# A state-space block and an FP4 feed-forward on one core: the rounded activations turned by DMA in bfloat16, their scales turned apart and repeated through DRAM

## The chip, the cores and the metric

The kernel runs on one core of a Trainium2 chip (trn2). The metric is device time in microseconds (us) for one launch. The kernel before takes 2007.83 us, the median of three runs that lie between 2003.05 and 2008.29 us. The profile was taken from one further execution, which took 2006.57 us.

## The reference

The input x is 8 sequences of 2048 tokens with 256 channels. The first half is a simplified Mamba layer (`xz = x @ W_in`, a causal convolution of 4 taps over 512 channels, SiLU, a small projection to 16 states, a mean over the sequence, a gate `silu(z)`, `@ W_out`), followed by a residual and a LayerNorm. The second half, which the change touches, is a gated feed-forward whose operands are all rounded to FP4 in blocks of 16 along the contraction:

```python
def fp4_quant_dequant(x):                       # blocks of 16 along the last dim
    scale = max(max|xb| / 6, 1e-12)
    return GRID[searchsorted(MID, |xb / scale|)] * sign(xb) * scale
def fp4_linear(x, w): return einsum('bsk,nk->bsn', fp4(x), fp4(w))
h = silu(fp4_linear(x, w_gate)) * fp4_linear(x, w_up)      # 256 -> 704
out = layernorm(x + fp4_linear(h, w_down))                 # 704 -> 256
```

So every activation that enters a feed-forward matmul is a grid value (at most 6, exact in bfloat16) times one scale for its block of 16.

## The kernel before, in words

**Tiles.** The sequence is cut into blocks of 512 tokens (`begin_block`, 32 of them), and each block into two pairs of 128-token tiles (`finish_pair`, 64 of them, m = 0 to 63). A block does the input projection (L408), the convolution taps on VectorE (L423), the state projection (L434) and its sums. `mix_block` (L521) adds the state's part four blocks later (`LAG = 4`). A pair does the gate branch z (L571), the output projection (L589), residual and LayerNorm, then the feed-forward: gate and up (L623), their product `h` (L638), down (L660), residual, LayerNorm, store.

**Rounding.** `quantize` (L164) has four steps. `scales` takes the maximum of each block (L180), a negative scale `nsc` (L184) and its reciprocal (L186), on VectorE. `normalize` multiplies on VectorE (L192) and takes the magnitude in bfloat16 on ScalarE (L199). `add` and `subtract` (L204, L208) round to the grid on VectorE. Last, GpSimd multiplies the rounded values by their scale (L209), in float32, in the layout [token, channel]. It is used for x1 (the LayerNorm's output, 2 x 256 columns a pair) and for h (2 x 704 = 1408 columns a pair), and for the three weights once.

**Turning.** TensorE contracts over partitions, so x1 and h must have channels on partitions. `turn_xq` (L604) makes four 128x128 TensorE transposes (L610) and one ScalarE copy out of PSUM (L612) for each pair. `turn_h` (L642) makes ten full transposes (L649) and two for the last 64 channels of each token tile (L652), with ScalarE copies L650 and L653. `down` (L655) then has twelve matmuls, six chunks of channels for each of two token tiles.

**Order.** Each step is put in a list by `at(place, f)`, where the places are constants at the top of the file (`GATE`, `QUANT2`, `HT`, `DOWN` ...), 64 of them to a block and 32 to a pair. The list is sorted and run, and a scheduler in the framework settles each engine's final order. Engines then work in order and wait on semaphores. All DMAs are issued from SP (SyncE), in order too. PSUM has seven banks in rotation (`bank`, L161). The drain at the end holds the four blocks of lag: there only pairs are left.

**Around the change.** `h`, the rounding scratch `q_x` and the convolution's `acc` have two or three buffers, and `x1`, `xq`, `r2` are separate tiles.

Of the kernel before, what the change touches and what calls it, by code (L numbers as in the profile page):

```python
# [8 lines left out]
F32 = mybir.dt.float32  # L9
BF16 = mybir.dt.bfloat16  # L10
# [17 lines left out]
CONV = (0.1, 17.0, 27.7, 51.2)  # L28
CONV_TAPS = 0.6
XPROJ = 66.0  # L30
TOKEN = 81.9
SOFTPLUS = 84.9
TURN = (75.4, 87.8, 88.5, 88.7)
SUMS = 93.4
SUM_LAG = 4.1
SKIP = 93.5
SKIP_STEP = 1.6
ZED = (24.8, 30.3)
MIX = 40.5
MIX_LAG = 2.2  # L40
MIX_STEP = 2.4
GATED = 13.9
GATED_LAG = 5.2
OUT = 59.5
NORM1 = 60.8
NORM_STEP = 4.3
QUANT1 = 86.5
QUANT1_STEP = 0.4
XQ = 90.2
GATE = (100.5, 104.5, 105.4)  # L50
PRODUCT_LAG = 5.5
QUANT2 = 118.6
QUANT2_STEP = 6.3
HT = 138.3
DOWN = 150.8
NORM2 = 160.8
PREPARE = (18.2, 50.1, 111.5, 171.7)
# [3 lines left out]
def mamba_fp4_ffn_kernel(  # L61
# [40 lines left out]
    ps_h = ctx.enter_context(tc.tile_pool(name="ps_h", bufs=1, space=PSUM))  # L102

# [16 lines left out]
    wdT = const.tile([P, NF + 1, DM], F32, name="wdT")  # L120

    hqT_of = [const.tile([P, NT * (NF + 1), P], F32, name=f"hqT{i}") for i in range(2)]
# [5 lines left out]
    nc.gpsimd.memset(wdT[TAIL:, NF, :], 0.0)  # L128
    for hqT in hqT_of:
        nc.gpsimd.memset(hqT[TAIL:, NT * NF :, :], 0.0)  # L130
# [33 lines left out]
    def quantize(place, v, q, n, step):  # L164

        nb = n // BLK
        state = {}

        def by_block(a):
            return a.rearrange("p (g k) -> p g k", k=BLK)

        def scales():
            amax = small.tile([P, nb], F32, tag="q_amax", name="q_amax")
            nc.vector.tensor_reduce(  # L180
                amax, by_block(v()), AX.X, ALU.max, apply_absolute_value=True
            )
            nsc = small.tile([P, nb], F32, tag="q_sc", name="q_sc")
            nc.vector.tensor_scalar(nsc, amax, -SIXTH, -1e-12, ALU.mult, ALU.min)  # L184
            rs = small.tile([P, nb], F32, tag="q_rs", name="q_rs")
            nc.vector.reciprocal(rs, nsc)  # L186
            state.update(nsc=nsc, rs=rs)

        def normalize():
            size, bufs = (T, 2) if n <= T else (NT * FF, 1)  # L190
            xn = fp4.tile([P, size], F32, tag=f"q_x{size}", name="q_x", bufs=bufs)[:, :n]
            nc.vector.tensor_tensor(  # L192
                by_block(xn),
                by_block(v()),
                state["rs"].unsqueeze(2).to_broadcast([P, nb, BLK]),
                ALU.mult,
            )
            w = fp4.tile([P, size], BF16, tag=f"q_w{size}", name="q_w", bufs=bufs)[:, :n]
            nc.scalar.activation(w, xn, AF.Abs, scale=GRID)  # L199
            state.update(x=xn, w=w)  # L200

        def add():
            xn, w = state["x"], state["w"]
            nc.vector.scalar_tensor_tensor(xn, w, 1.5 * GRID, xn, ALU.max, ALU.subtract)  # L204

        def subtract():
            xn, w = state["x"], state["w"]
            nc.vector.scalar_tensor_tensor(w, w, 1.5 * GRID, xn, ALU.max, ALU.subtract)  # L208
            nc.gpsimd.tensor_tensor(  # L209
                by_block(q()),  # L210
                by_block(w),
                state["nsc"].unsqueeze(2).to_broadcast([P, nb, BLK]),
                ALU.mult,
            )

        for i, f in enumerate((scales, normalize, add, subtract)):
            at(place + i * step, f)

    def prepare_gate_up(place, w, wT):
        wv = {}  # L220

        def load():
            wv["w"] = p2.tile([P, NF, DM], F32, tag="h", name="wv")
            nc.sync.dma_start(wv["w"], w[: NF * P, :].rearrange("(j p) d -> p j d", p=P))
# [5 lines left out]
        quantize(place + 0.5, flat, flat, NF * DM, 1.0)  # L230
# [18 lines left out]
    def prepare_gate_up_tail(place):  # L249
# [3 lines left out]
        def load():  # L253
            wv["w"] = p2.tile([P, DM], F32, tag="h", name="wt")
            nc.sync.dma_start(wv["w"][:TAIL], w_gate[NF * P :, :])
            nc.sync.dma_start(wv["w"][TAIL:], w_up[NF * P :, :])

        at(place, load)
        quantize(place + 0.5, lambda: wv["w"], lambda: wv["w"], DM, 0.5)
# [17 lines left out]
    def prepare_down(place):  # L277
        wv = {}

        def load():  # L280
            wv["w"] = p2.tile([P, KM, FF], F32, tag="h", name="wdv")
            nc.sync.dma_start(wv["w"], w_down.rearrange("(r p) f -> p r f", p=P))

        def flat():
            return wv["w"].rearrange("p r f -> p (r f)")

        at(place, load)
        quantize(place + 0.5, flat, flat, KM * FF, 1.0)

        def turn(r):  # L290
            cols = slice(r * P, (r + 1) * P)
            for j0, j1 in ((0, 4), (4, NF)):
                tp = bank()
                for j in range(j0, j1):
                    nc.tensor.transpose(
                        tp[:, (j - j0) * P : (j - j0 + 1) * P],
                        wv["w"][:, r, j * P : (j + 1) * P],
                        ident,
                    )
                nc.scalar.copy(  # L300
                    wdT[:, j0:j1, cols],
                    tp[:, : (j1 - j0) * P].rearrange("p (j n) -> p j n", n=P),
                )
            tp = bank()
            nc.tensor.transpose(tp[:TAIL, :P], wv["w"][:, r, NF * P :], ident)
            nc.scalar.copy(wdT[:TAIL, NF, cols], tp[:TAIL, :P])

        for r in range(KM):
            at(place + 9.0 + 2 * r, turn, r)
# [77 lines left out]
    def begin_block(n):  # L387
# [9 lines left out]
        def project(c):  # L397
# [3 lines left out]
            xp = s["xp"] = p3.tile([P, HALO + T], F32, tag="xp", name="xp")  # L401
# [16 lines left out]
            acc = s["acc"] = p3.tile([P, T], F32, tag="acc", name="acc")  # L418
            nc.scalar.activation(acc, xp[:, 0:T], AF.Copy, scale=cw_sb[:, c, 0:1])  # L419

        def tap(c, k):
            acc, xp = s["acc"], s["xp"]
# [3 lines left out]
            if k == KC - 1:  # L426
                nc.scalar.activation(s["xc"][:, c, :], acc, AF.Silu, bias=cb_sb[:, c : c + 1])  # L427
# [120 lines left out]
    def finish_pair(m):  # L548
# [52 lines left out]
        def make_xq():  # L601
            q["xq"] = p2.tile([P, NT * DM], F32, tag="xq", name="xq")

        def turn_xq():  # L604
            tp = bank()
            xq = q["xq"].rearrange("p (t d) -> p t d", d=DM)
            for k in range(KM):
                for t in range(NT):
                    o = k * U + t * P
                    nc.tensor.transpose(tp[:, o : o + P], xq[:, t, k * P : (k + 1) * P], ident)  # L610
            q["xqT"] = p2.tile([P, KM, U], F32, tag="xqT", name="xqT")
            nc.scalar.copy(q["xqT"].rearrange("p k t -> p (k t)"), tp)  # L612

        def gate_up(f0):
            if f0 == 0:
                q["h"] = p2.tile([P, NT, FF], F32, tag="h", name="h")
            n = min(FW, FF - f0)
            gu = []
            for wT in (wgT, wuT):
                mm = bank().rearrange("p (t n) -> p t n", n=FW)  # L620
                for t in range(NT):
                    for k in range(KM):
                        nc.tensor.matmul(  # L623
                            mm[:, t, :n],
                            q["xqT"][:, k, t * P : (t + 1) * P],
# [16 lines left out]
        def turn_h():  # L642
            h, hT = q["h"], hqT_of[m % 2]
            cols = [h[:, t, j * P : (j + 1) * P] for t in range(NT) for j in range(NF)]
            for j0 in range(0, len(cols), 4):
                j1 = min(j0 + 4, len(cols))
                tp = bank().rearrange("p (j n) -> p j n", n=P)
                for j in range(j0, j1):
                    nc.tensor.transpose(tp[:, j - j0, :], cols[j], ident)  # L649
                nc.scalar.copy(hT[:, j0:j1, :], tp[:, : j1 - j0, :])  # L650
            for t in range(NT):
                nc.tensor.transpose(tp[:TAIL, NT + t, :], h[:, t, NF * P :], ident)  # L652
            nc.scalar.copy(hT[:TAIL, NT * NF :, :], tp[:TAIL, NT:, :])  # L653

        def down():  # L655
            hT = hqT_of[m % 2]
            mm = q["d"] = bank().rearrange("p (t n) -> p t n", n=DM)
            for t in range(NT):
                for j in range(NF + 1):
                    nc.tensor.matmul(  # L660
                        mm[:, t, :],
                        hT[:, t * NF + j if j < NF else NT * NF + t, :],
                        wdT[:, j, :],
# [4 lines left out]
        def residual2():  # L668
            q["r2"] = p2.tile([P, NT, DM], F32, tag="r2", name="r2")
            nc.vector.tensor_tensor(q["r2"], q["x1"], q["d"], ALU.add)  # L670

        def store():
            nc.sync.dma_start(of[b, i], q["r2"])
# [3 lines left out]
        for j in range(2):  # L677
# [5 lines left out]
        at(base + QUANT1 - 0.1, make_xq)  # L683
        quantize(
            base + QUANT1,
            lambda: q["x1"].rearrange("p t d -> p (t d)"),
            lambda: q["xq"],
            NT * DM,
            QUANT1_STEP,
        )  # L690
        at(base + XQ, turn_xq)
# [7 lines left out]
        quantize(base + QUANT2, flat, flat, NT * FF, QUANT2_STEP)  # L699
        at(base + HT, turn_h)  # L700
        at(base + DOWN, down)
        at(base + NORM2, residual2)
        layernorm(base + NORM2 + 0.5, lambda: q["r2"], lambda: q["r2"], NORM_STEP)
# [11 lines left out]
    prepare_down(PREPARE[3])  # L715
# [49 lines left out]
```

## Time and profile before

| | |
|---|---|
| runs, median (range) | 2007.83 us (2003.05 to 2008.29) |
| the profiled execution, whole | 2006.57 us |
| its span | 2004.6 us |
| TensorE matmuls (PE) busy | 1952.9 us, 97% |
| TensorE weight loads (PEld) | 1586.8 us, 79% |
| VectorE (DVE) | 1534.9 us, 77% |
| ScalarE (ACT) | 992.8 us, 50% |
| GpSimd (POOL) | 663.3 us, 33% |
| DMA, mean share of 16 engines | 11.1%, 72.92 MB moved |
| TensorE clock granted | 0.992 of full |

The span runs from the first to the last instruction, and the remaining 2 us lie around it. A busy time is the union of an engine's instructions. The profile's matmul rows give pipelined durations whose ends are modelled, so a matmul's share of time is better read from the starts of neighbours in the timeline than from its mean. Each float32 matmul instruction of the program appears as two records in it, a transpose as one. In the groups, `out<-in` names the tiles, the number after x counts instructions, and what follows the second bar is the idle time of the engine ahead of them with what ended it.

### The profile page before, as it was taken

To read this page: it belongs to the slowest core of one execution; us is meant where nothing else is said; L and a number is where in the kernel's file an instruction comes from. 1 tells how busy PE (TensorE), PEld (TensorE's weight loads), DVE (VectorE), ACT (ScalarE), POOL (GpSimd) and SP (SyncE) were. 2 spreads that over 40 slices of the span, in tenths; PEclk is the share of its full clock that TensorE was granted. 3 is DMA by queue.
4 is the path that set the end of the run, shared out by engine and by line. 5 is a ranking of instruction groups with operands and counts; after the bars stand their busy time and mean duration, and the time that the engine had idled before them with its cause. 6 is when DMAs were issued, how large, how long until landed. Compare 5 with 4: busy or idle time off the path is not lost.

```text
span 2004.6 us, 31117 instructions
## 1 busy us (share of the span) xinstructions
PE 1952.9 (97%) x12146; PEld 1586.8 (79%) x12146; DVE 1534.9 (77%) x2938; ACT 992.8 (50%) x1764; POOL 663.3 (33%) x658
## 2 busy tenths in 40 slices
PE   5799999999999999999999999999999999999997
PEld 2468888888888888888888888888888888888886
DVE  6878777887777877777777777777777877767775
ACT  4755545455544455444455444555445555433332
POOL 2224323423333323333233432333323333333331
PEclk8999999999999999999999999999999999999998
DMA  4011111101111110011011011011011011011100
GB/s 129 32 39 36 32 38 43 38 32 32 32 38 43 34 36 32 27 43 43 29 35 39 27 43 43 27 33 43 27 43 40 30 33 32 17 32 32 37 13 20
DMA packets 66290, 72.92 MB, mean 36 GB/s; under 512 B 6112, under 2 KB 57184, under 8 KB 66144
## 3 DMA queue, kind: packets, MB, share of 16 engines
q1 hardware_dynamic: 66144, 70.94, 11.1%
q8 instruction: 96, 1.57, 0.3%
q14 instruction: 50, 0.41, 0.1%
HBM read 54.15 MB, written 16.78 MB: 35 GB/s over the span
## 4 chain that ended last, share of the span: by engine, by line
PE 93%; DVE 4%; POOL 1%; ACT 1%; issue 0%; DMA 0%; SPq 0%; POOLq 0%; ACTq 0%; DVEq 0%
PE ps L623 31%; PE ps L660 16%; PE ps L571 11%; PE ps L589 11%; PE ps L408 10%; PE ps L649 3%; PE ps L434 3%; PE ps L465 2%; PE ps L532 2%; PE hsum L475 2%; PE ps L610 1%; DVE acc L423 1%; PE ps L652 1%; DVE q_x L192 0%; DVE q_amax L180 0%
## 5 line engine op out<-in xcount | busy, mean ns | idle before, releaser
L660 PE MATMUL ps<-wdT,hqT 128*128 128x256 f32 x1536 | 345.9, 380 | 0.5 <-ACT hqT L650 0.3
L623 PE MATMUL ps<-wgT,xqT 128*128 128x256 f32 (+1 forms) x1536 | 341.7, 365 | 0.7 <-ACT xqT L612 0.7
L623 PE MATMUL ps<-wuT,xqT 128*128 128x256 f32 (+1 forms) x1536 | 335.6, 361 | 0.0
L660 PEld LDWEIGHTS ps<-wdT,hqT 128*128 128x128 f32 x1536 | 288.6, 190 | 51.6 <-issue 6.2
L623 PEld LDWEIGHTS ps<-wgT,xqT 128*128 128x128 f32 x1536 | 276.4, 190 | 39.7 <-ACT x L373 5.0
L423 DVE SCALAR_TENSOR_TENSOR acc<-xp,cw_sb,acc 128x512 f32<-128x512 f32 x384 | 288.4, 753 | 24.3 <-ACT acc L419 11.1
L623 PEld LDWEIGHTS ps<-wuT,xqT 128*128 128x128 f32 x1536 | 279.5, 190 | 26.5
L408 PE MATMUL ps<-xT,w_in_sb 128*128 128x512 f32 x512 | 254.0, 603 | 6.2 <-DMA xT<-in_x_t_dram 6.2
L571 PE MATMUL ps<-xTz,w_in_sb 128*128 128x256 f32 x1024 | 245.0, 382 | 0.0
L589 PE MATMUL ps<-w_out_sb,xc 128*128 128x256 f32 x1024 | 231.6, 379 | 0.0
L571 PEld LDWEIGHTS ps<-xTz,w_in_sb 128*128 128x128 f32 x1024 | 189.9, 190 | 48.6 <-issue 25.3
L582 POOL TENSOR_TENSOR xc<-xc,sz 128x512 f32<-128x512 f32 x128 | 166.2, 1309 | 154.7 <-ACT sz L578 88.9
L632 ACT ACTIVATE sg<-ps 128x512 f32<-128x512 f32 (+1 forms) x192 | 106.7, 556 | 217.9 <-PE ps L623 217.9
L589 PEld LDWEIGHTS ps<-w_out_sb,xc 128*128 128x128 f32 x1024 | 189.6, 190 | 23.2
L427 ACT ACTIVATE xc<-acc,cb_sb 128x512 f32<-128x512 f32 x128 | 92.4, 722 | 222.5 <-DVE acc L423 222.5
L209 POOL TENSOR_TENSOR h<-q_w,q_sc 128x1408 f32<-128x1408 bf16 x64 | 165.4, 2584 | 107.1 <-DVE q_w L208 82.8
L204 DVE SCALAR_TENSOR_TENSOR q_x<-q_w,q_x 128x1408 f32<-128x1408 bf16 (+2 forms) x132 | 153.2, 1160 | 56.9 <-ACT q_w L199 56.5
L638 DVE TENSOR_TENSOR h<-sg,ps 128x512 f32<-128x512 f32 (+1 forms) x192 | 122.8, 640 | 89.3 <-PE ps L623 86.6
L405 POOL COPY xp<-halo 128x3 f32<-128x3 f32 x96 | 78.6, 818 | 323.2 <-DVE acc L423 175.1
L578 ACT ACTIVATE sz<-ps 128x512 f32<-128x512 f32 x128 | 75.8, 592 | 184.9 <-PE ps L571 184.9
L199 ACT ACTIVATE q_w<-q_x 128x1408 bf16<-128x1408 f32 (+2 forms) x132 | 132.3, 1003 | 56.5 <-DVE q_x L192 53.8
L208 DVE SCALAR_TENSOR_TENSOR q_w<-q_w,q_x 128x1408 bf16<-128x1408 bf16 (+2 forms) x132 | 153.5, 1163 | 0.6
(101 smaller groups left out, 2586.9 us busy)
## 6 DMA issues: line engine op xcount, KB each, us to landing
xT<-in_x_t_dram SPq DMA_DIRECT2D x32, 512.0 KB, 3.6
xTz<-in_x_t_dram SPq DMA_DIRECT2D x64, 256.0 KB, 2.9
xt<-in_L_attn_x_dram SPq DMA_DIRECT2D x64, 256.0 KB, 2.7
out_dram<-r SPq DMA_DIRECT2D x64, 256.0 KB, 2.1
w_in_sb<-in_L_attn_W_in_dram SPq DMA_DIRECT2D x2, 512.0 KB, 4.2
wdv<-in_L_ffn_w_down_dram SPq DMA_DIRECT2D x1, 704.0 KB, 4.1
wv<-in_L_ffn_w_gate_dram SPq DMA_DIRECT2D x1, 640.0 KB, 6.9
wv<-in_L_ffn_w_up_dram SPq DMA_DIRECT2D x1, 640.0 KB, 9.2
```

The source lines that it names most:

```text
L199: nc.scalar.activation(w, xn, AF.Abs, scale=GRID)
L204: nc.vector.scalar_tensor_tensor(xn, w, 1.5 * GRID, xn, ALU.max, ALU.subtract)
L208: nc.vector.scalar_tensor_tensor(w, w, 1.5 * GRID, xn, ALU.max, ALU.subtract)
L209: nc.gpsimd.tensor_tensor(by_block(q()), by_block(w), state["nsc"].unsqueeze(2).to_broadcast([P, nb, BLK]), ALU.mult,)
L408: nc.tensor.matmul(mm, w_in_sb[:, k, c * P : (c + 1) * P], s["xT"][:, k, :], start=(k == 0), stop=(k == KM - 1),)
L423: nc.vector.scalar_tensor_tensor(acc, xp[:, k : k + T], cw_sb[:, c, k : k + 1], acc, ALU.mult, ALU.add)
L571: nc.tensor.matmul(mm[:, j, :], w_in_sb[:, k, DI + (c + j) * P : DI + (c + j + 1) * P], q["xT"][:, k, :], start=(k == 0), stop=(k == KM - 1),)
L582: nc.gpsimd.tensor_tensor(xc, xc, q["sz"][:, c : c + 2, :], ALU.mult)
L589: nc.tensor.matmul(mm[:, t, :], s["xc"][:, c, o : o + P], w_out_sb[:, c, :], start=(c == 0), stop=(c == NC - 1),)
L623: nc.tensor.matmul(mm[:, t, :n], q["xqT"][:, k, t * P : (t + 1) * P], wT[:, k, f0 : f0 + n], start=(k == 0), stop=(k == KM - 1),)
L638: nc.vector.tensor_tensor(q["h"][:, :, f0 : f0 + n], sg[:, :, :n], up[:, :, :n], ALU.mult)
L660: nc.tensor.matmul(mm[:, t, :], hT[:, t * NF + j if j < NF else NT * NF + t, :], wdT[:, j, :], start=(j == 0), stop=(j == NF),)
```

## The change

- `quantize` is split. Its rounding becomes `round_fp4`, and the weights still use it with the GpSimd multiply as before. x1 and h use a new `quantize_turned`.
- There the rounded, unscaled grid values (bfloat16) are turned by one DMA transpose from SBUF to SBUF (4 blocks of 128 columns for x1, 11 for h).
- The scales, [128 tokens, 32 or 88 blocks], are turned by one small TensorE transpose and copied out of PSUM by ScalarE. One DMA writes them to DRAM 16 times each, a second DMA reads them back so that each channel's partition has the scale of its block.
- GpSimd then multiplies on the turned side, float32 scales with bfloat16 values.
- `turn_xq` and `turn_h` are gone. h is turned as 11 whole chunks over the two token tiles, so the middle chunk holds the last 64 channels of the first tile and the first 64 of the second; `wdT` becomes two tiles, one for each token tile, padded with zero rows to fit. `down` keeps twelve matmuls. The down weights are prepared in two halves.
- `h` and `q_x` get one buffer each, `acc` is worked in place in `xc`, and the second residual is made in place in `x1`.
- All places at the top of the file have new values.

```diff
+    dram = ctx.enter_context(tc.tile_pool(name="dram", bufs=2, space=bass.MemoryType.DRAM))
...
-    wdT = const.tile([P, NF + 1, DM], F32, name="wdT")
+    wdT = [const.tile([P, NF + 1, DM], F32, name=f"wdT{t}") for t in range(NT)]
...
+    def quantize_turned(place, v, n, step, spread_lag, turn_lag, qT):
+        state = round_fp4(place, v, n, step)
+        nb, chunks = n // BLK, n // P
+        def turn_scales():
+            tp = bank()
+            nc.tensor.transpose(tp[:nb, :P], state["nsc"], ident)
+            scT = p2.tile([P, P], F32, tag="q_scT", name="q_scT")
+            nc.scalar.copy(scT[:nb, :], tp[:nb, :P])
+            rows = dram.tile([nb, BLK, P], F32, tag=f"q_rows{n}", name="q_rows")
+            nc.sync.dma_start(rows, scT[:nb, :].unsqueeze(1).to_broadcast([nb, BLK, P]))
+            state["rows"] = rows
+        def spread_scales():
+            state["scT"] = fp4.tile([P, chunks, P], F32, tag=f"q_s{n}", name="q_s", bufs=1)
+            nc.sync.dma_start(
+                state["scT"], state["rows"].rearrange("(c b) k n -> (b k) c n", c=chunks)
+            )
+        def turn():
+            state["gT"] = fp4.tile([P, chunks, P], BF16, tag=f"q_gT{n}", name="q_gT", bufs=1)
+            nc.sync.dma_start_transpose(state["gT"], state["g"])
+        def scale():
+            nc.gpsimd.tensor_tensor(qT(), state["gT"], state["scT"], ALU.mult)
...
-        def turn_xq():
...
-                    nc.tensor.transpose(tp[:, o : o + P], xq[:, t, k * P : (k + 1) * P], ident)
...
-                            q["xqT"][:, k, t * P : (t + 1) * P],
+                            q["xqT"][:, t * KM + k, :],
...
-        def turn_h():
...
-                    nc.tensor.transpose(tp[:, j - j0, :], cols[j], ident)
...
-                        hT[:, t * NF + j if j < NF else NT * NF + t, :],
-                        wdT[:, j, :],
+                        q["hqT"][:, t * NF + j, :],
+                        wdT[t][:, j, :],
```

## The prediction

> **What bounds the kernel now.** I read the engines' busy shares first, then busy time by stretch, then the groups of instructions with shapes kept apart, then TensorE's timeline in a steady stretch and at the end, and last the DMA issues.
>
> ```profile
> span 2004.6 us, 31117 instructions
> PE 1952.9 (97%) x12146; PEld 1586.8 (79%) x12146; DVE 1534.9 (77%) x2938; ACT 992.8 (50%) x1764; POOL 663.3 (33%) x658
> PE   5799999999999999999999999999999999999997
> ```
> ```profile
> 512.00:1024.00 512.00, 512.00 (x3224) 418.56 (x3224) 394.58 (x767) 258.40 (x461) 174.41 (x170) 1.00 0.11 35
> ```
>
> The columns of the second fence are length, then PE, PEld, DVE, ACT and POOL, clock, DMA share. In the middle PE has no gap at all (512.00 of 512.00) at full clock, while DVE works 77% and the DMA engines 11%. PE is idle only at the head (36.7 us in the first 128, from the same view's rows) and at the end (15 us in the last 85). So a PE instruction removed from the middle is time removed, as long as nothing new arrives late.
>
> ```profile
> L649 PE MATMUL ps<-ident,h 128*128 128x128 f32 x640 | 81.5, 275 | 6.2 <-POOL h L209 6.2
> L610 PE MATMUL ps<-ident,xq 128*128 128x128 f32 x256 | 38.5, 273 | 0.0
> L652 PE MATMUL ps<-ident,h 128*64 128x128 f32 x128 | 25.4, 280 | 0.1
> L209 POOL TENSOR_TENSOR h<-q_w,q_sc 128x1408 f32<-128x1408 bf16 x64 | 165.4, 2584 | 107.1 <-DVE q_w L208 82.8 <-DVE sp_acc L332 14.8 <-DVE sp_acc L337 5.8
> L582 POOL TENSOR_TENSOR xc<-xc,sz 128x512 f32<-128x512 f32 x128 | 166.2, 1309 | 154.7 <-ACT sz L578 88.9 <-DVE xc L542 59.5 <-DVE ln_mv L361 4.1
> ```
> ```profile
> 1014.87 1.25 PE L649 MATMUL ps<-ident,h 128*128 128x128 f32 x10
> 1015.96 0.60 PE L465 MATMUL ps<-ident,xc 128*128 128x128 f32 x4
> ...
> 1026.78 0.60 PE L610 MATMUL ps<-ident,xq 128*128 128x128 f32 x4
> 1027.21 3.62 PE L589 MATMUL ps<-w_out_sb,xc 128*128 128x256 f32 x16
> ```
>
> A transpose's mean of 275 ns overlaps its neighbours. What it takes is the distance of starts: ten in 1015.96 - 1014.87 = 1.09 us, four in 0.43 us, so 0.109 us each.
>
> **What PE loses and gains.** Removed: 640 + 256 + 128 = 1024 transposes x 0.109 = 111.6 us. Added: one scale transpose for x1 and one for h in each pair, again 128 moving columns, 128 x 0.109 = 14.0 us. Net -97.6 us, 1.53 us a pair. `down` keeps twelve matmuls a pair, gate and up are unchanged. The steady time of a pair falls from 30.1 us (two in 60.2, from the timeline) to 28.6.
>
> DVE has the same instructions, 394.58 us of the former 512, that is 82% of the shorter period: no bound. ACT loses five copies a pair and gains two small ones. In-place `acc`, `x1` and single `h`, `q_x` cost nothing: writer and earlier reader stand in order on DVE, or DVE has already waited for that ACT reader.
>
> **What is new on the path.** The built order of each engine gives the distances: I summed PE's instructions between two places with the spacing above (256-column matmul 0.432 us, 192 columns 0.325, 512 columns 0.88). In a steady pair there are
> - 20.3 to 21.0 us of PE work from x1's scale transpose to the first gate matmul,
> - 22.3 to 22.7 us from h's scale transpose to `down`,
> - 29.6 to 30.7 us (30.1) from the last up matmul to `down`.
>
> SP issues, a pair: turn of x1, row write of x1, its read, row write of h, turn of h, its read, then the loads xt and xTz, then the store; every second pair has an xT load in between. SP waits at each read until the write has landed, and at each turn for DVE; the loads have a period or more of cover (xTz is used 39 us later), and so has the store (four buffers of x1).
>
> ```profile
> xT<-in_x_t_dram SPq DMA_DIRECT2D x32, 512.0 KB, 3.6
> xTz<-in_x_t_dram SPq DMA_DIRECT2D x64, 256.0 KB, 2.9
> ...
> cw_sb<-in_L_attn_conv_w_dram SPq DMA_DIRECT2D x1, 8.0 KB, 4.6
> ```
> ```profile
> q1 hardware_dynamic: 66144, 70.94, 11.1%
> ```
>
> xT and xTz both have 256 pieces; 256 KB more cost 0.7 us, so about 2.2 us are fixed and bytes go at 370 KB/us. A packet takes 0.111 x 2004.6 x 16 / 66144 = 54 ns of an engine on average, for 1.07 KB. The new row DMAs have pieces of 512 bytes: 512 for x1, 1408 for h, each way. By bytes h's 704 KB take 2.2 + 1.9 = 4.1 us. At 54 ns a piece the read takes 2.2 + 88 x 0.054 = 7.0. [...] I take 6.5 for the write, 5.5 for the read, between the ends; for x1 3.4 each.
>
> The transpose DMA is shown by no row. By bytes 352 KB take 2.2 + 1.0 = 3.2 us; as 1408 pieces of 256 bytes at 54 ns, 7.0. [...] The cw row, 512 tiny pieces in 4.6 us, says too that small pieces aren't cheap. I take 5 us for h and 3 for x1, nearest to the rows of loads, with 3.2 below and 12 or more above.
>
> GpSimd's multiply now reads two full operands: 2.58 us if like L209, 1408/512 x 1.31 = 3.6 if like L582. I take 3.1; POOL stays under 40%.
>
> - x1, scales: copy 0.3 + write 3.4 + read 3.4 + multiply 1.2 + hand-overs 0.5 = 8.8 against 20.3: covered.
> - h, scales: 0.3 + 6.5 + 5.5 + 3.1 + 0.5 = 15.9 against 22.3: covered[...].
> - h, values: SiLU 0.5, product 0.6, block maximum to rounding 1.62 + 0.21 + 0.70 + 1.63 + 1.38 + 1.63 + 1.62 = 8.8, three taps and the residual between them 3.0, hand-overs 0.5: 13.4. Then turn 5 + the read that SP has put behind it 5.5 + multiply 3.1 + 0.5 = 27.5 against 30.1: covered by 2.6.
>
> DMA load: 3840 pieces at 27 to 54 ns over 16 engines is 6.5 to 13 us, turns 2 to 8, loads 3.5: 12 to 24 us of 28.6.
>
> **Where cover is missing.** In the drain PE has only 22 to 23 us between up and `down`, and the values' chain without taps is 25.2: 2.8 us late at worst for six pairs. I book 8 us, between 0 and 17.
>
> ```profile
> 1977.20 4.48 PE L660 MATMUL ps<-wdT,hqT 128*128 128x256 f32 x20
> 1987.86 2.39 PE L649 MATMUL ps<-ident,h 128*128 128x128 f32 x10 [6.18 <-POOL h L209]
> ```
>
> At the very end PE idled 6.2 us for h's multiply. In the new order h's scale transpose stands behind the `down` of the pair before, so the last two pairs each show the scale chain: about 6 us (15.9 less one gate and up of 9.8), then 15.9 bare, 5 to 6 for an earlier pair and x1's chain, 7.3 for the last norm and store: 34 against 15 before. I book +18 (10 to 27). Head: one buffer for `h` makes the weight preparations queue up; +2 (-5 to +10), since it waits for DMA and DVE anyway.
>
> Sum against the profiled execution's 2006.6: -97.6 + 8 + 18 + 2 = 1937. The runs' median is 1.2 us higher, below the sum's grain.
>
> **Rivals.**
> 1. *Every 512-byte piece costs the full 54 ns* and the multiply 3.6. Steady pairs stay covered (values 13.4 + 5 + 7.0 + 4.1 = 29.5). Drain +21, the two bare scale chains +9: 1967. For it: the small-piece row; against: the mean packet is twice as large.
> 2. *The turn itself is too slow, and `down` waits for it in every pair.* Place: GpSimd's multiply of h, with SP's read queued behind the turn. At 12 us the chain is 34.5, 4.4 over; a stall also moves the next pair's chain, so x 28.35/30.1 = 0.94. 56 steady pairs x 4.4 x 0.94 = 232, drain +51, end +10: 2230, slower. It decides at 8.5 us: past 7.6 each us costs 53 + 6, and 55 are left there. [...]
> 3. *No effect*, late data eating just the 70 us: a turn within half a us of 8.5.
>
> **Chances.** Forecast 0.52 (1905 to 1957; a 7 us turn is still inside), rival 1 0.16, rival 2 0.28, rival 3 0.04. A measurement tells about 0.3% from no change: faster 0.68, same 0.04, slower 0.28. The range must reach into rival 2, whose upper part is open: 1900 to 2160 leaves out about 0.02 below and 0.17 above. Both signs hold much, so beside it the forecast's own 1905 to 1957.
>
> **What would show it.** PE's steady pair at 28.6 us with no idle ahead of `down`; transposes landing in 3 to 7 us; writes of h 4 to 9, reads 4 to 7; PE idle some 20 us more at the end. Wrong if waits on the multiply for the turn appear ahead of `down` or gate in the middle, or the DMA share passes 0.8.

## The result, and the profile after

The changed kernel takes 1977.57 us (median of 4 runs, 1972.72 to 1978.70) against 2007.70 us of the kernel before, a ratio of 0.985 (95% interval 0.983 to 0.987): 1.5% faster. The prediction was 1937 us. Its direction held; of the 70 us that it expected, 30 came. The profiled execution took 1978.70 us.

From the page of the changed kernel, in order: span, busy times, PE's and the clock's tenths in 40 slices, and the DMA queue (packets, MB, share).

```profile
span 1976.9 us, 30190 instructions
...
PE 1865.9 (94%) x11262; PEld 1503.3 (76%) x11262; DVE 1612.6 (82%) x2944; ACT 882.5 (45%) x1575; POOL 730.8 (37%) x660
...
PE   3789999999999999999999999999999999999983
...
PEclk7799999999999999999999999999999999999997
...
q1 hardware_dynamic: 442672, 228.26, 52.6%
```

PE has lost 87 us of busy time (1952.9 to 1865.9) and the span only 27.7. So PE now stands idle for some 60 us more. Two places show in the tenths: the first three slices (3, 7, 8 where 5, 7, 9 stood) and the last (3 where 7 stood). The third can't be seen in tenths. The stretch from 512 to 1024 us shows it (length, then PE, PEld, DVE, ACT, POOL, clock, DMA share, GB/s):

```profile
512.00:1024.00 512.00, 509.72 (x3129) 412.50 (x3129) 441.59 (x813) 239.99 (x431) 199.88 (x180) 1.00 0.57 123
```

PE had 512.00 there. DVE has gone from 394.58 to 441.59 with no new kind of work.

To place the loss I took the start of each pair's first `down` matmul from PE's timeline and subtracted the kernel before. Minus is earlier than before; a few matmul records are missing from the traces, which moves single starts but not these differences by more than about half a microsecond.

| first `down` of pair | before, us | after, us | after - before |
|---|---|---|---|
| 0 | 172.9 | 197.0 | +24.2 |
| 16 | 656.4 | 661.3 | +4.9 |
| 32 | 1139.9 | 1123.9 | -15.9 |
| 56 | 1841.0 | 1796.2 | -44.8 |
| 59 | 1914.5 | 1865.9 | -48.6 |
| 63 | 1990.5 | 1962.8 | -27.8 |

Four stages, then: the head loses 24.2 us, the 56 pairs after it gain 69.0 (1.23 a pair, where 1.53 were expected), the drain gains 3.8, and the last four pairs lose 20.8. Behind the last `down` both take 14.1 us.

**The head.** PE's waits in the first 200 us (engine, tile and line, releaser: us in total, times, longest). First before, then after:

```profile
PE ps L238 <- POOL wv L209: 18.1, 2, 15.6
...
PE ps L295 <- POOL wdv L209: 1.9, 1, 1.9
```
```profile
PE ps L283 <- POOL wv L219: 19.2, 2, 15.7
PE ps L339 <- POOL wdv L219: 8.0, 2, 7.5
```

L238 and L295 of the kernel before, L283 and L339 of the changed one, are the weight preparations' transposes. SP's issue of the up weight's load (start, time on the issuing queue), before and after:

```profile
8.31 0.47 SPq L224 DMA_DIRECT2D wv<-in_L_ffn_w_up_dram  x1
```
```profile
28.16 0.37 SPq L269 DMA_DIRECT2D wv<-in_L_ffn_w_up_dram  x1
```

The rounding of that weight begins at 20.20 us before and at 32.42 after: its tile now has the one buffer of `h`, and that holds the gate weight until PE has turned it (at 28.09). The second half of the down weight waits in the same way, and its transposes stand on PE ahead of block 2's convolution: PE is idle for 7.47 us before them, they start at 89.83 us, and the next input projection (L442) follows at 92.45. In the first three stretches of 32 us PE is busy for 10.1, 19.4 and 21.2 us where it was for 10.3, 26.1 and 25.8, and the clock granted to it is 0.73, 0.74 and 0.78 where it was 0.79, 0.95 and 0.95 (PEclk above, 7 in the first two slices). If PE's time there goes with the clock, its 40.6 us from 32 to 96 would be about 8 us shorter at 0.95. That is an estimate; no run changes the clock alone.

**The middle.** PE's waits from 256 to 1700 us. Before there were none; after there is this one line:

```profile
PE ps L648 <- DVE h L663: 12.2, 14, 1.1
```

Gate's matmul (L648) waits for a PSUM bank that VectorE frees with `h` (L663). Why VectorE is late shows in the timeline (start, duration, engine and line, and in brackets the idle time and what ended it):

```profile
1029.04 2.94 POOL L257 TENSOR_TENSOR hqT<-q_gT,q_s 128x1408 f32<-128x1408 bf16 x1 [5.29 <-ACT sg L657]
...
1029.29 3.25 DVE L208 SCALAR_TENSOR_TENSOR q_w<-q_w,q_x 128x512 bf16<-128x512 bf16 x1
...
1032.45 1.27 DVE L663 TENSOR_TENSOR h<-sg,ps 128x512 f32<-128x512 f32 x2
...
1033.18 1.57 PE L648 MATMUL ps<-wgT,xqT 128*128 128x192 f32 x8 [0.73 <-DVE h L663]
```

VectorE's rounding step of x1 starts 0.25 us after GpSimd's new multiply and takes 3.25 us. The same step took 0.69 before. GpSimd ends at 1031.98, VectorE at 1032.54. The two rows of x1's rounding, shapes kept apart, before and after:

```profile
L204 DVE SCALAR_TENSOR_TENSOR q_x<-q_w,q_x 128x512 f32<-128x512 bf16 x64 | 44.3, 692 | 41.1 <-ACT q_w L199 40.7
...
L208 DVE SCALAR_TENSOR_TENSOR q_w<-q_w,q_x 128x512 bf16<-128x512 bf16 x64 | 43.9, 686 | 0.5
```
```profile
L204 DVE SCALAR_TENSOR_TENSOR q_x<-q_w,q_x 128x512 f32<-128x512 bf16 x64 | 97.9, 1530 | 39.3 <-ACT q_w L199 38.5
...
L208 DVE SCALAR_TENSOR_TENSOR q_w<-q_w,q_x 128x512 bf16<-128x512 bf16 x64 | 85.7, 1340 | 0.5
```

A mean of 1.5 us is a mixture. Alone, the steps take 677 to 693 ns, as before. Of all 128, 42 take over 1 us (3336 ns at most), and these together cost VectorE 95 us more than they did. The records show how. All 42 began while a GpSimd multiply of x1 or h was running, and they end 548 ns after it (10th to 90th percentile 546 to 551). None of the 19 that began before the multiply beside them was held, and none of the other 67. Where a VectorE step of this kind began first, GpSimd's multiply was the longer one: h's, 2.88 us alone, took up to 3.40, and x1's, 1.17 alone, up to 2.62 (beside a step of 1408 columns). By these records the two do not share a rate: of such a pair, the one that begins second ends late by about what was left of the other. Before, the places kept x1's rounding and GpSimd's multiplies apart: none of the 128 was over 0.7 us.

The kernel before had the same hold in another place, in the softplus:

```profile
L337 DVE SCALAR_TENSOR_TENSOR sp_acc<-sp_acc,sp_s 128x4 f32<-128x4 f32 x224 | 88.1, 393 | 6.5
```

Of these 224 small steps, 26 took 2.1 us where the rest took about 0.16, and all 26 ended within 22 ns after GpSimd's multiply of h. The new order moved them away from it (mean 165 ns), which gave VectorE some 51 us back. So its busy time rose by 78 us only.

**The end.** The last three `down` of the changed kernel on PE:

```profile
1912.68 8.12 PE L671 MATMUL ps<-wdT,hqT 128*128 128x256 f32 x24 [4.54 <-POOL hqT L257]
...
1938.14 7.34 PE L671 MATMUL ps<-wdT,hqT 128*128 128x256 f32 x24 [7.73 <-POOL hqT L257]
...
1962.75 6.99 PE L671 MATMUL ps<-wdT,hqT 128*128 128x256 f32 x24 [17.16 <-POOL hqT L257]
```

4.5 + 7.7 + 17.2 = 29.4 us of waiting for the turned h, where 6.2 were lost before.

**The DMAs.** SP's issues in one steady pair of the changed kernel, of h's scale write, h's turn and h's scale read (start, time on the issuing queue):

```profile
1014.56 0.88 SPq L243 DMA_DIRECT2D q_rows<-q_scT  x1
1018.04 4.09 SPq L254 DMA_TRANSPOSE q_gT<-q_w  x1
1023.37 0.38 SPq L248 DMA_DIRECT2D q_s<-q_rows  x1
```

The turn holds SP for 4.1 us and lands 6.8 us after its issue starts (median of the landing semaphores, 5.1 to 8.5 from the 10th to the 90th percentile). The read is issued 8.7 us after the write (median): SP waits there until the write has landed (197.1 us in 121 waits of SP for these writes over the whole kernel; the read is issued 0.02 us after h's write has landed, median). It lands 5.3 us later. GpSimd's multiply of h ends 4.2 us (median) before `down` begins. So the chain that the prediction feared most is covered in the steady pairs: PE has no wait for the turned h from 256 to 1700 us.

### The profile page after: what moved, and what is told of

Read it like the earlier page. It is cut to its first block, busy times and chain, and to the rows that moved or that the text cites. A ratio compares the mean times of both kernels' runs of the same rounds, so it can differ in the third digit from the quotient of the medians.

```text
span 1976.9 us, 30190 instructions
## 1 busy us (share of the span) xinstructions
PE 1865.9 (94%) x11262; PEld 1503.3 (76%) x11262; DVE 1612.6 (82%) x2944; ACT 882.5 (45%) x1575; POOL 730.8 (37%) x660
## 3 DMA queue, kind: packets, MB, share of 16 engines
q1 hardware_dynamic: 442672, 228.26, 52.6%
## 4 chain that ended last, share of the span: by engine, by line
PE 66%; DVE 16%; DMA 8%; POOL 4%; issue 3%; ACT 2%; SPq 1%; POOLq 0%; ACTq 0%; DVEq 0%
PE ps L648 22%; PE ps L671 13%; PE ps L606 8%; PE ps L624 8%; PE ps L442 8%; DVE xc L458 4%; DMA q_rows<-q_scT 4%; DMA q_s<-q_rows 3%; PE ps L469 2%; DVE q_x L204 2%; PE ps L500 2%; DVE q_amax L180 2%; DVE q_w L208 1%; POOL sp_e L356 1%; POOL hqT L257 1%
## 5 line engine op out<-in xcount | busy, mean ns | idle before, releaser
L648 PE MATMUL ps<-wgT,xqT 128*128 128x256 f32 (+1 forms) x1536 | 341.7, 365 | 12.7 <-DVE h L663 12.6
L648 PE MATMUL ps<-wuT,xqT 128*128 128x256 f32 (+1 forms) x1536 | 336.7, 362 | 1.4 <-DVE h L663 1.4
L458 DVE SCALAR_TENSOR_TENSOR xc<-xp,cw_sb,xc 128x512 f32<-128x512 f32 x384 | 295.4, 771 | 30.7 <-ACT xc L452 28.1
L257 POOL TENSOR_TENSOR hqT<-q_gT,q_s 128x1408 f32<-128x1408 bf16 x64 | 190.7, 2979 | 336.5 <-DMA q_s<-q_rows 261.3
L648 PEld LDWEIGHTS ps<-wgT,xqT 128*128 128x128 f32 x1536 | 274.4, 190 | 50.8 <-DVE h L663 15.4
L648 PEld LDWEIGHTS ps<-wuT,xqT 128*128 128x128 f32 x1536 | 280.5, 191 | 28.5 <-DVE h L663 2.0
L442 PE MATMUL ps<-xT,w_in_sb 128*128 128x512 f32 x512 | 247.4, 608 | 6.2 <-DMA xT<-in_x_t_dram 6.2
L204 DVE SCALAR_TENSOR_TENSOR q_x<-q_w,q_x 128x1408 f32<-128x1408 bf16 (+3 forms) x133 | 214.7, 1614 | 43.0 <-ACT q_w L199 42.2
L617 POOL TENSOR_TENSOR xc<-xc,sz 128x512 f32<-128x512 f32 x128 | 190.9, 1502 | 143.1 <-ACT sz L613 69.4
L199 ACT ACTIVATE q_w<-q_x 128x1408 bf16<-128x1408 f32 (+3 forms) x133 | 132.6, 997 | 206.6 <-DVE q_x L192 184.6
L208 DVE SCALAR_TENSOR_TENSOR q_w<-q_w,q_x 128x1408 bf16<-128x1408 bf16 (+3 forms) x133 | 211.3, 1588 | 0.8
L407 ACT ACTIVATE x<-x,ln_nb,ln_rs 128x256 f32<-128x256 f32 x256 | 141.6, 594 | 137.6 <-DVE ln_nb L405 137.5
L442 PEld LDWEIGHTS ps<-xT,w_in_sb 128*128 128x128 f32 x512 | 95.6, 196 | 80.0 <-issue 74.6
L257 POOL TENSOR_TENSOR xqT<-q_gT,q_s 128x512 f32<-128x512 bf16 x64 | 96.5, 1508 | 132.1 <-DMA q_s<-q_rows 96.0
```

The lines of the kernel that those rows point to most:

```text
L257: nc.gpsimd.tensor_tensor(qT(), state["gT"], state["scT"], ALU.mult)
L407: nc.scalar.activation(dst()[:, t, :], r()[:, t, :], AF.Identity, bias=nb[:, t : t + 1], scale=rstd[:, t : t + 1],)
L442: nc.tensor.matmul(mm, w_in_sb[:, k, c * P : (c + 1) * P], s["xT"][:, k, :], start=(k == 0), stop=(k == KM - 1),)
L458: nc.vector.scalar_tensor_tensor(acc, xp[:, k : k + T], cw_sb[:, c, k : k + 1], acc, ALU.mult, ALU.add)
L617: nc.gpsimd.tensor_tensor(xc, xc, q["sz"][:, c : c + 2, :], ALU.mult)
L648: nc.tensor.matmul(mm[:, t, :n], q["xqT"][:, t * KM + k, :], wT[:, k, f0 : f0 + n], start=(k == 0), stop=(k == KM - 1),)
```

## The experiments

Four theories. A: the head is late for the one staging buffer. B: it is late for the new places of the preparations. C: VectorE's two-operand steps are held by GpSimd's multiplies. D: the last pairs show the bare chain of turn, scale write and scale read. Each run's ratio is to the kernel before on the same chip; its medians there lie between 2006.7 and 2007.8 us, so that the runs' times can be compared too.

**1. The old places for the preparations** (theory B)

```diff
-PREPARE = (3.2, 57.2, 100.3, 150.2)
+PREPARE = (18.2, 50.1, 111.5, 171.7)
```

> The changed kernel with the four start places of the weight preparations set back to those of before (18.2, 50.1, 111.5, 171.7). The changed kernel's first down matmul starts 24 us later than before. Theory A (the single buffer of the staging tile makes each weight load wait until the weight before it has been turned, and TensorE stands behind the late weight): places alone give back little, at most 10 us: first down at 187 us or later, time 1968 to 1978. Theory B (the new places put the weight transposes ahead of convolution work on TensorE): the head comes back nearly whole, first down near 175 us, time about 1956.

Measured: 1971.68 us, ratio 0.983 [0.981, 0.984]. The first `down` is still 22.4 us late. B falls as the cause of the head; the places are worth some 6 us in this kernel.

**2. Other staging buffers** (theory A). The up weight is staged in a `wdT` tile that is filled later, the second half of the down weight in the tile of h's scales.

```diff
-            wv["w"] = p2.tile([P, NF, DM], F32, tag="h", name="wv", bufs=1)
+            if w is w_up:
+                wv["w"] = wdT[0][:, :NF, :]
+            else:
+                wv["w"] = p2.tile([P, NF, DM], F32, tag="h", name="wv", bufs=1)
...
+                wide = fp4.tile([P, NT * FF], F32, tag=f"q_s{NT * FF}", name="wdv2", bufs=1)
+                wv["w"] = wide[:, : TAIL + FF + TAIL]
```

> The changed kernel with its own places, but the up weight staged in the down weight's tile, which is still empty then, and the second half of the down weight staged in the tile of the spread scales, so that no staging load waits for the turn of the weight before it. Theory A (one staging buffer): first down back to about 178 us, time 1957 to 1963. Theory B (places): first down stays at 190 or later, time above 1970.

Measured: 1959.31 us, ratio 0.977 [0.975, 0.978]: 18 us less than the changed kernel. The first `down` is 9.6 us late instead of 24.2, and PE's wait for the down weight's rounding is 4.1 us instead of 8.0. Theory A's own figure was a first `down` at 178 us; it came at 182.5. A is confirmed for about 15 of the head's 24 us. This kernel is the base of the next runs.

**3. Both together**

> Both edits to the weight preparation. Theory A and theory B both give a first down at 172 to 178 us and a time of 1953 to 1960; if it stays above 1970, the late head comes from the other places (convolution, taps), not from the weights.

Measured: 1964.31 us, ratio 0.979 [0.977, 0.980], first `down` 10.7 us late (at 183.6 us). Both theories' figures are missed, 172 to 178 us and 1953 to 1960. The old places add nothing to the buffers. What is left of the head, 5 to 11 us in this and later runs, stays open.

**4. No scale DMAs.** The multiply takes a constant tile of ones, which leaves the scales of x1 and h out of the result; their write and read are gone, the turns stay.

```diff
-            state["scT"] = fp4.tile([P, chunks, P], F32, tag=f"q_s{n}", name="q_s", bufs=1)
-            nc.sync.dma_start(
-                state["scT"], state["rows"].rearrange("(c b) k n -> (b k) c n", c=chunks)
-            )
+            state["scT"] = ones[:, :chunks, :]
```

> The changed kernel without the two scale DMAs: the scales are still turned and copied, but the multiply takes a constant tile of ones, so the scale is left out of the result. It takes away 123 MB of DMA traffic and the write-and-read chain. If the end's loss of 21 us is the bare scale chain, it shrinks by 12 to 18 us, and the middle, where that chain is covered, stays at 28.4 us a pair: time 1958 to 1966. Rival: the traffic itself (the DMA engines' share of 53%) slows the middle; then the pair falls to the sum's 28.6 minus waits, that is by 0.2 us or more, and the time comes under 1950.

Measured: 2038.85 us, ratio 1.016 [1.015, 1.018], slower than before, with less work. No theory foresaw it. The waits of that kernel tell what happened:

```profile
POOL xqT L253 <- DMA q_gT<-q_w: 331.9, 54, 9.5
POOL hqT L253 <- DMA q_gT<-q_w: 305.8, 58, 11.5
...
DVE ln_nb L401 <- POOL ln_rs L395: 208.7, 128, 7.2
```

With no scales to wait for, the scheduler put GpSimd's multiplies earlier, just behind the turn's issue. GpSimd then stands waiting for the turn (331.9 and 305.8 us) with LayerNorm's small `ln_rs` behind it, VectorE waits for that (208.7 us in all, 87.0 in the changed kernel), and ScalarE for VectorE (345.1 us ahead of L403, where the changed kernel has 137.5). As a removal of a cost the run is void, since the order changed with it. It shows what the wait costs in the wrong place on a queue.

**5. GpSimd's multiply in pieces** (theory C), on run 2's base:

```diff
+PIECE = 3
...
-            nc.gpsimd.tensor_tensor(qT(), state["gT"], state["scT"], ALU.mult)
+            for c0 in range(0, chunks, PIECE):
+                c = slice(c0, min(c0 + PIECE, chunks))
+                nc.gpsimd.tensor_tensor(qT()[:, c], state["gT"][:, c], state["scT"][:, c], ALU.mult)
```

> The kernel of the run with other staging buffers (1959.3, ratio 0.977), with GpSimd's multiply on the turned side cut in pieces of 3 chunks (128x384)[...]; the work is the same, four instructions for one at h. Theory C (VectorE's rounding steps with two operands in SBUF are held until GpSimd's multiply is through): the longest 128x512 step of L208 falls from about 3.3 us to 1.2 or less, PE's waits for VectorE's h vanish in the middle, every second pair goes from about 29.9 to 29.2, and the time is 1940 to 1950. Rival (the half microsecond of every second pair is VectorE's order or an issue, not GpSimd): steps and pairs stay, 1957 to 1962; if GpSimd's own extra starts cost more than the pieces free, it is 1960 to 1968.

Measured: 1933.30 us, ratio 0.963 [0.962, 0.964]: 26 us less than run 2, and 7 us below the range that was expected. x1's rounding is nearly back to its old means, though GpSimd itself works more (727 to 818 us):

```profile
L209 DVE SCALAR_TENSOR_TENSOR q_w<-q_w,q_x 128x512 bf16<-128x512 bf16 x64 | 53.3, 832 | 0.5
L205 DVE SCALAR_TENSOR_TENSOR q_x<-q_w,q_x 128x512 f32<-128x512 bf16 x64 | 50.4, 788 | 39.3 <-ACT q_w L200 38.5
```

The longest is 1.33 us. PE waits for nothing from 256 to 1700 us. Pairs alternate 28.0 and 29.1 us where they took 28.0 and about 29.8, and the mean of pairs 8 to 56 is 28.09 against 29.72 before the change: 1.62 us a pair, a little more than the 1.53 that PE's sum gave. Of the 30 us between the two profiled executions 5 lie ahead of the first `down`, 18 in the 56 pairs behind it, and 7 in the last four pairs. C holds for the middle. At the end the pieces may have a second effect, `down` beginning on the first chunks while GpSimd works on the last; the runs don't show it apart from the first.

**6. No multiply of h on GpSimd.** ScalarE copies instead, which leaves h's scale out of the result. The base is run 2's again.

```diff
-            nc.gpsimd.tensor_tensor(qT(), state["gT"], state["scT"], ALU.mult)
+            if n > T:
+                nc.scalar.copy(qT(), state["gT"])
+            else:
+                nc.gpsimd.tensor_tensor(qT(), state["gT"], state["scT"], ALU.mult)
```

> The kernel of the run with other staging buffers (1959.3), with the multiply of h on GpSimd replaced by a copy on ScalarE, which leaves h's scale out of the result (its two scale DMAs still run). Theory C: GpSimd no longer stands beside VectorE's rounding steps with its longest operation, L208 and L204 at 128x512 come back from means of 1.3 and 1.5 us to 0.7 to 0.9, VectorE's busy time falls by 50 to 70 us, pairs alternate 28.0 and 29.2, and the time is 1935 to 1950. Rival: the longer steps come from DMA traffic in SBUF, which is the same here: they stay over 1.2 us and the time is 1955 to 1962.

Measured: 2037.91 us, ratio 1.016 [1.014, 1.018]. The durations are as C said: x1's two steps have means of 692 and 689 ns, none over 0.7 us, and the same scale and turn DMAs run. DMA traffic is thus not what stretched them. The time is a miss, for the reason of run 4 on another engine:

```profile
ACT hqT L258 <- DMA q_gT<-q_w: 448.1, 64, 11.1
```

ScalarE waits for the turn in every pair, and what others need from it comes behind: VectorE was idle for 171.3 us ahead of x1's block maximum for ScalarE's norm, and for 119.5 ahead of the convolution's taps (28.5 and 28.1 in the changed kernel).

**7. The last two pairs on TensorE** (theory D), on run 2's base. `quantize_on_pe` is the scheme of the kernel before: scale, four transposes to a bank, a ScalarE copy. x1 of these two pairs gets it in the same way (`LAST_X`).

```diff
+LAST_H, LAST_X = 62, 62
...
+        if m >= LAST_H:
+            quantize_on_pe(base + QUANT2, flat, NT * FF, QUANT2_STEP, lambda: q["hqT"])
+        else:
+            quantize_turned(
```

> The kernel of the run with other staging buffers (1959.3), with x1 and h of the last two pairs (62, 63) scaled before the turn and turned on TensorE as in the kernel before. Theory D (the bare chain of turn, scale write and scale read at the end is what the last pairs lose): the loss from the 59th to the 63rd down, 20 us, shrinks to 3 to 8, and the time is 1942 to 1950. Rival (the end is late for VectorE's and ScalarE's own steps, which are the same either way): the loss stays within 4 us of 20 and the time is 1955 to 1962.

Measured: 1943.10 us, ratio 0.968 [0.967, 0.970], 16 us less than run 2. From the 59th to the 63rd `down` it loses 6.9 us instead of 20.0. PE's waits for the turned h at the end are 7.4 us, where run 2 had 31.6. D is confirmed.

**8. h turned twice**, the second time into a tile that nobody reads, on run 2's base:

```diff
             nc.sync.dma_start_transpose(state["gT"], state["g"])
+            if n > T:
+                again = fp4.tile([P, chunks, P], BF16, tag="q_again", name="q_again", bufs=1)
+                nc.sync.dma_start_transpose(again, state["g"])
```

> The kernel of the run with other staging buffers (1959.3), with h turned twice, the second time into a tile that only that turn writes; the multiply can wait for the first alone. By the prediction's point of decision (8.5 us for h's turn, about 4.6 us a pair behind 14 us): if the second turn stands in the way of the first like a longer one, 64 x 5 us = 2250 to 2290. By the measured landing (the first turn lands 4 us before the scales do, and the multiply ends 5.7 us before down begins): the second lies behind the first on the queue and delays only the scale read that follows it by 4 to 7 us, so 1960 to 2000.

Measured: 1958.04 us, ratio 0.976 [0.974, 0.977], the same as run 2 and 2 us below the lower of the two ranges. The timeline of SP shows where the second turn went:

```profile
1020.84 0.89 SPq L243 DMA_DIRECT2D q_rows<-q_scT  x1
1024.25 4.28 SPq L254 DMA_TRANSPOSE q_gT<-q_w  x1
1028.59 1.76 SPq L257 DMA_TRANSPOSE q_again<-q_w  x1
1030.45 0.53 SPq L248 DMA_DIRECT2D q_s<-q_rows  x1
```

Write to read is 9.6 us here (median 9.7, against 8.7). The second turn fills a time in which SP waited for the write anyway, so it delays the read by 1 us, and the multiply still ends 2.8 us before `down`. That adding 64 turns of h cost nothing is partly luck: VectorE's and GpSimd's steps moved a little against each other, and only 22 of x1's rounding steps were held for over 1 us instead of run 2's 39.

**9. The pieces alone**, on the changed kernel itself, with its one staging buffer:

> The changed kernel itself with the pieces alone, one staging buffer and all turns by DMA as before. If head and contention are separate causes, it gains on 1977.6 what the pieces gained on the other staging buffers (26 us): 1948 to 1956, with a first down still 22 to 25 us late, pairs at 28.0 and 29.1 in the middle, and no wait of PE for VectorE's h there. Rival (the gain of the pieces came from the other order that they gave VectorE and SyncE at the head): 1965 to 1978.

Measured: 1946.27 us, ratio 0.970 [0.968, 0.971], 31 us less than the changed kernel, 2 us below the range. The first `down` is 23.9 us late as in the changed kernel, pairs alternate 28.0 and 29.1, and PE waits for nothing in the middle. Head and middle are separate causes. What goes beyond run 5's 26 us lies in the last four pairs, which lose 8.7 us here and 13.1 in run 5; why is open.

**10. Buffers, pieces and the last two pairs together** (the edits of runs 2, 5 and 7)

> Other staging buffers, pieces of 3 chunks in GpSimd's multiply, and the last two pairs turned on TensorE, together. If the three causes are separate, the last pairs' loss from the 59th to the 63rd down falls from 13.2 us (pieces alone) to about 5, with pairs at 28.0 and 29.1 in the middle: 1933 less 8 to 14, 1919 to 1926, ratio 0.957 to 0.960. Rival (the pieces had already shortened the end by what the turn on TensorE saves): 1929 to 1934.

Measured: 1920.00 us, ratio 0.956 [0.954, 0.957]: 58 us less than the changed kernel and the best version found. The steps 18.3 (buffers, run 2), 26.0 (pieces, run 5) and 13.3 (the last two pairs) make it up in this order; pieces alone gave 31 in run 9, so the gains don't quite add.

**11. As run 10, x1 of every pair on TensorE**

```diff
-LAST_H, LAST_X = 62, 62
+LAST_H, LAST_X = 62, 0
```

> As the run with all three, but x1 of every pair is scaled before the turn and turned on TensorE as in the kernel before; h alone goes by DMA (to pair 61). TensorE gets 8 times 0.109 less one turn of scales of 0.109 back for each pair, 0.76 us by the prediction's rate of a turn of 128x128 in float32 alone; x1 is 4 of the 15 turns of a sequence, so 4 x 0.109 - 0.109 = 0.33 us a sequence and pair: 62 x 0.33 = 20 us more than the run with all three, 1938 to 1948. Rival (x1's chain by DMA costs VectorE and GpSimd as much as it saves TensorE): within 4 us of the run with all three.

Measured: 2092.20 us, ratio 1.042 [1.041, 1.044], a miss by 150 us. PE's one wait from 256 to 1700 us:

```profile
PE ps L683 <- ACT xqT L287: 90.6, 46, 2.6
```

The turn stood on PE directly ahead of gate, so 46 of the gates in that stretch waited for ScalarE's copy of `xqT`. Of the 172 us above run 10 this wait is 91 and PE's added transposes 20 by their rate; the rest was not traced. I had kept x1's late places, made for a chain of DMAs.

**12. The same with x1's rounding called earlier**

```diff
-QUANT1_STEP = 7.9
+QUANT1_STEP = 4.0
```

> The run with x1 turned on TensorE (2092.2 us) again, with x1's rounding steps called earlier (QUANT1_STEP 4.0 for 7.9), so that its turn stands ahead of the z and output projections and not just ahead of gate, where TensorE waited 90.6 us for the copy of xqT. If that place was the loss, the wait is gone, and what is left over the run with all three (1920.0) is TensorE's own work, four transposes less one for each of 62 pairs, 62 x 3 x 0.109 = 20 us: 1938 to 1950. Rival (x1's turn on TensorE costs as such, whatever its place): 1990 or more.

Measured: 1939.67 us, ratio 0.966 [0.965, 0.968], and PE waits for nothing in the middle. It is 19.7 us above run 10, for 20 that three transposes a pair at 0.109 us give. Pairs take 28.3 and 29.4 where run 10 has 28.0 and 29.1. So the rate of a transpose was right, and turning x1 by DMA is worth its 20 us once nothing else is late.

x1's rounding steps (L204 and L208 of the changed kernel, 128 in all) and the middle of the kernel, side by side:

| kernel | of the 128, over 1 us | their excess over 0.69 us, all 128 | mean pair, 8 to 56 | PE's waits for `h`, 256 to 1700 us |
|---|---|---|---|---|
| before | 0 | 0 us | 29.72 us | 0 |
| after | 42 | 95.4 | 28.43 | 12.2 us |
| run 2, other buffers | 39 | 85.2 | 28.38 | 9.8 |
| run 8, turned twice | 22 | 51.6 | 28.29 | 1.8 |
| run 5, pieces | 17 | 15.3 | 28.09 | 0 |

The fewer and shorter the held steps, the shorter the pair, down to what PE's own work takes.

## Why the prediction was right or wrong

Put into the table's stages, the prediction had +2 for the head, 56 x 1.525 = -85.4 for the middle, and +13.8 for all that follows (8 pairs at -1.525, +8 for the drain, +18 for the end). Measured: +24.2, -69.0, +17.0. The misses are 22, 16 and 3 us, together the 42 us between -70 and -27.7.

1. **PE's sum: right.** 1024 transposes less 128 at 0.109 us. Where nothing else is late (run 5) the pair shrinks by 1.62 us for 1.53; run 12 gives the rate once more.
2. **The head: the step that failed most.** "One buffer for `h` makes the weight preparations queue up; +2 (-5 to +10), since it waits for DMA and DVE anyway." The mechanism was named and the cover was not looked at. Before, the up weight's load ran beside the gate weight's rounding. With one buffer it comes after that weight's turn, and on PE the late transposes hold up the convolution behind them (7.47 us of idle time ahead of those of the down weight's second half). Measured +24.2 for +2, of which run 2 takes back 14.6 at the first `down` and 18.3 in all; the cause of the rest is open.
3. **"DVE has the same instructions, 394.58 us of the former 512 ... no bound": wrong.** The instructions were the same, their durations were not. The prediction moved GpSimd's multiply to another place and costed its own duration (3.1 us, measured 2.98), but not what it does to VectorE beside it. The kernel before showed it in its softplus steps, 2.1 us for 0.16 and ended within 22 ns after GpSimd's multiply, and the prediction did not look there. In the changed kernel 0.69 us becomes up to 3.34, ending 0.55 after GpSimd, in all 42 steps that began second and in none that began first. From the softplus steps and the durations in the prediction's own rows (0.69 and 2.58 us), an estimate of up to 3.3 us could have been booked for each of x1's two steps where the orders let them meet. And a busy share of 82% says nothing about one late step: the bank that gate needs is freed by the next operation in VectorE's queue. Runs 5, 6 and 9 show it, at about 16 of the 42 us.
4. **The end and the drain: right together.** In PE's waits for the turned h, the last three `down` lost 29.4 us where 6.2 were lost before: 23 us for the +18 (10 to 27) that was booked for the bare chains, and run 7 takes 13 of it back. The three other waits of the drain come to 4.5 us, for +8 (0 to 17). So 28 us stand against 26; the table's +20.8 and -3.8 are smaller by what PE saves in these seven pairs. That the two misses cancel is luck.
5. **The DMAs: right.** Turn of h 5 us (3.2 to 7.0), measured 6.8; read of h 5.5, measured 5.3; write of h 6.5 (4 to 9), measured 8.7 to the read's issue, near the upper end, which was the author's assumption and stood on no row; x1's turn 3, measured 2.5, its write and read 3.4, measured 3.2 and 2.9. Mean time of a 512-byte piece 32 ns, within 27 to 54. The DMA share went to 52.6% with PE's middle not waiting for any landing.
6. **The rivals.** The slow turn (rival 2) did not come: the 12 us that it supposed, which no row had shown, are excluded by 6.8 (5.1 to 8.5). Its point of decision at 8.5 us was wrong as well. The sum put the read behind the turn; the trace has the read behind the landing of the write, with the turn beside it, and run 8 puts a second turn there for nothing. The prediction's upper range reached so far for a danger that had more cover than it counted. Rival 1's 1967 is nearer to the measured 1978 than the forecast, for another reason: the 512-byte pieces took 32 ns each, not 54.

What stays open: 5 to 11 us of the head, how much of the head's loss is the lower clock, and how the gain of GpSimd's pieces in the last pairs, 7 us (run 5) to 12 us (run 9), divides between VectorE's held steps and an earlier start of `down`.

## What to carry to other kernels

When an operation moves to another engine or another time, list what will run beside it and whether the trace already shows the two holding each other: here a GpSimd multiply of two SBUF operands cost VectorE 95 us in 42 held steps while its own end stayed 4.2 us (median) ahead of `down` in the steady pairs, and cutting it in pieces of three chunks, an edit of a few lines, took PE's waits in the middle away and gave 31 us (run 9). A buffer count taken down for space in the steady state is paid in the head, where loads run ahead (24.2 us here, 14.6 of them back with other buffers), so follow the first tile's loads through it. In a chain of DMAs, ask what each issue waits for before summing: in this one the wait for the write's landing (8.7 us from its issue) hid the turn beside it, which held SP for 4.1 us. And put no wait ahead of small work that others need: on GpSimd, ScalarE and PE that work came behind the wait, which went with a loss of some 60, 80 and 150 us in runs 4, 6 and 11.

## What the runs showed of the hardware

- In the changed kernel a step of x1's rounding (L204, L208: two tensors in SBUF, 128x512) that began on VectorE while a GpSimd multiply ran ended 0.55 us after it and took up to 3.34 us for 0.69 (42 of 42 steps, within 5 ns between the 10th and 90th percentile). One that began first was not held (0 of 19), and the multiply was lengthened instead (h's up to 3.40 us for 2.88; x1's up to 2.62 for 1.17, beside a step of 1408 columns).
- The block maximum (L180, 1620 ns alone and beside) and operations with an operand in PSUM (`h` L663, 677 ns alone and 683 beside; L577, 677 and 680) were not held. Steps of 128x1408 (L208) went from 1614 to 2165 ns beside a multiply, and a 128x2 step with one input (L397) from 156 to 1164 in 31 of 128 cases, as it did in the kernel before (1243, 33 cases). The first step of the rounding (L192, one operand broadcast) kept its 1620 ns for h in all 20 cases beside a GpSimd operation, and in all of them VectorE had begun first; for x1 it took 3367 instead of 690 in the two cases where the multiply had.
- A DMA transpose of 128x1408 bfloat16 from SBUF to SBUF took 6.8 us with 4.1 on the issuing queue, one of 128x512 2.5 and 1.2. Two in a row on one queue didn't add up in run 8: the second needed 2.0 us of issue (median, 1.6 to 2.5) and landed 4.9 us after its issue began.
- A write to DRAM from 88 partitions, 704 KB in 512-byte pieces, took about 8.7 us, the read of the same bytes to 128 partitions 5.3.
